# A conditional transformer chain on one core: tables with neutral rows, and a new order for late weights and masks

## The chip, the cores and the metric

The kernel runs on one core of a Trainium2 chip. A core has five engines with an instruction queue each: PE (matrix products), DVE (vector work), ACT (activations), POOL (GpSimd) and SP (here only for asking for transfers). Each engine takes its instructions in order. Sixteen DMA engines move data; transfers are asked for on the queues of SP, ACT and POOL. The metric is the time of one execution in device microseconds, the median of several runs.

## The reference

Four stages are applied one after the other to x, sixteen batch entries b of 256 tokens by 256 channels, in float32.

- Stage 0, an adapter with an expert for each b: `hidden = gelu(x @ down_W.T + down_b)`, then `hidden @ expert_W[id].T + expert_b[id]` where the id is valid (otherwise hidden is kept), plus an embedding, then `@ up_W.T + up_b`, plus x, and a layer norm with gain and offset.
- Stage 1, a transformer block with 16 heads of 16 channels: layer norm with a scale and a shift that come from a timestep (sine, cosine, silu, a 256x512 product); q, k, v; scores plus a bias of its own for every head (`fside`, 16 heads x 256 x 256 for each b), masked, softmax; projection; then a feed-forward net of 1024 channels with `x * sigmoid(1.702 x)`.
- Stage 2, one of three small nets for each b (two with two products, one with three), chosen by a condition 0, 1 or 2; nothing is added where the condition is something else; then a layer norm with gain and offset.
- Stage 3, one step of a two-dimensional finite-difference scheme: the field is multiplied by grids, differentiated along both axes (with one-sided forms at the edges), scaled by a dt for each b, added and clipped at zero.

In the inputs that are used every expert id and condition is valid, and condition 2 does not occur.

## The kernel before

Everything is done for one b after the other, with 128 rows on the partitions. Eight generators describe the stages: `prepare` (stage 0), `project` (q, k, v), `weigh` (scores, bias, softmax), `attend` (transposed probabilities times values, then `divide` and the projection), `enter` and `feed` (the feed-forward net), `end` (stage 2) and `step` (stage 3). A planner, `Flow`, runs when the program is built: it keeps an estimated clock for each engine and goes on with the generator that is ready and has the lowest position; `flow.add(gen, at, per)` gives each its starting position and how fast it advances. The order in which generators are resumed is the order of the instructions on each engine. Several stages of different b therefore interleave on PE.

In `weigh` the heads are taken in quads, 64 quads in all, four for each b. For each quad `load_side` asks SP for the 1 MB of biases (`side`, three buffers), and `add_mask` asks POOL for a transfer that adds the spread mask `neg` (made by `spread_mask` from the loaded mask) to the biases in place (L632). The softmax (L675 on DVE, exp at L686 on ACT) waits for that transfer. Before, quads 1 and 2 get their masks when quad 0 has been weighed, and quad m + 2 at the third head of quad m. `prepare` for b = 0 calls `timestep` after the first statistics and `condition` after the second ones.

Weights that are used later (w1, rows_b, w2, w_sr, grids: L185 on SP) are asked for at the start, behind the biases of quads 0 to 2. Expert weights are loaded by the id of each b (L279), and made neutral for an invalid id on POOL: multiplied by a valid flag (L486), and a diagonal `e_k` (L281) is added (L487). Branch weights of stage 2 are loaded by condition (L909), their last bias is multiplied by a valid flag (L989), and the product is multiplied by it as it is added (L1041).

`take_stats` makes mean and variance on DVE (L387, L388), and on POOL the inverse root `rs` (L391, L392) and `nb`, minus mean times rs (L394, L395). `normalized` applies them either on DVE (L402, without nb) or on ACT (L407, with nb), whichever engine's estimated clock is behind.

Of the kernel before, what the change touches and what calls it, by code (L numbers as in the profile page):

```python
# [11 lines left out]
F32 = mybir.dt.float32  # L12
BF16 = mybir.dt.bfloat16
I32 = mybir.dt.int32
# [5 lines left out]
P = 128  # L20
# [150 lines left out]
def chain_kernel(ctx: ExitStack, tc: tile.TileContext, t: dict, out: bass.AP):  # L171
# [57 lines left out]
    e_rows = load("e_rows", t["expert_rows"], [E, 2 * A])  # L229
# [21 lines left out]

    def steer(name, tok, n):

        f = fixed(f"{name}_f", [P, B])
        nc.vector.tensor_copy(f, tok)
        clip = fixed(f"{name}_clip", [P, B])
        nc.vector.tensor_scalar(clip, f, 0.0, float(n - 1), ALU.max, ALU.min)
        clip_i = fixed(f"{name}_clip_i", [P, B], I32)
        nc.vector.tensor_copy(clip_i, clip)
        valid = fixed(f"{name}_valid", [P, B])  # L260
        nc.vector.tensor_tensor(valid, clip, f, ALU.is_equal)
        return clip, clip_i, valid

    e_clip, e_idx, e_valid = steer("e", tok[:, :B], E)
    e_hot = small()
    nc.vector.tensor_scalar(e_hot, e_clip, columns("number"), None, ALU.is_equal)
    e_hot_valid = small()
    nc.vector.tensor_tensor(e_hot_valid, e_hot, e_valid, ALU.mult)

    e_keep = fixed("e_keep", [A, B])  # L270
    nc.vector.tensor_scalar(e_keep, e_valid[:A], -1.0, 1.0, ALU.mult, ALU.add)
# [3 lines left out]
    def load_expert(b):  # L275

        e = nc.sync.value_load(e_idx[0:1, b : b + 1], min_val=0, max_val=E - 1)
        w = xp.tile([A, A], F32, name=f"e_w{b}", tag="e_w")
        nc.sync.dma_start(out=w, in_=t["expert_W"][bass.ds(e, 1)].rearrange("e a o -> a (e o)"))  # L279
        keep = xp.tile([A, A], F32, name=f"e_k{b}", tag="e_k")  # L280
        nc.gpsimd.tensor_scalar(keep, ident[:A, :A], e_keep[:, b : b + 1], None, ALU.mult)  # L281
        e_ws[b] = w, keep

    load_expert(0)
    HB = 4
    sides = {}

    def load_side(m):
# [45 lines left out]
    def timestep():  # L334
# [4 lines left out]
        flow.dve(1.8)  # L339
        flow.act(3.5)  # L340
# [19 lines left out]

    load_mask(0)
    load_side(0)
# [3 lines left out]
    def later(name, src, shape):  # L366
        return load(name, src, shape, engine=nc.sync)

    load_side(1)
    wo = later("wo", chunked(t["Wo"]), [P, NC, D])  # L370
    load_side(2)
    w1 = later("w1", chunked(t["W1"]), [P, NC, F])
    rows_b = later("rows_b", rows(t["rows_b"]), [P, 3 * D + B])
    b2, ln3_g, ln3_b = (rows_b[:, i * D : (i + 1) * D] for i in range(3))
    dt = rows_b[:, 3 * D :]
    w2 = later("w2", chunked(t["W2"]), [P, NF, D])
    w_sr = later("w_sr", chunked(t["w_sr"]), [P, 6, D])
    w1_sr, w2_sr = w_sr[:, :NC, :], w_sr[:, NC:, :]
    grids = later("grids", chunked(t["grids"]), [P, NC, 7 * S])
# [3 lines left out]
    def take_stats(name, src, after):  # L383
# [9 lines left out]
        nb = xp.tile([P, NC], F32, name=f"nb{name}", tag="nb", bufs=12)  # L393
        nc.gpsimd.tensor_tensor(nb, mv[:, :, 0], rs, ALU.mult)  # L394
        nc.gpsimd.tensor_scalar(nb, nb, -1.0, None, ALU.mult)  # L395
        return (mv, rs, nb), flow.pool(1.65, at)

    def normalized(dst, src, stat):
        mv, rs, nb = stat
        if flow.clock["DVE"] <= flow.clock["ACT"]:  # L400
# [4 lines left out]
            return flow.dve(0.65)  # L405
        for c in range(NC):
# [3 lines left out]
        return flow.act(0.97)  # L410
# [47 lines left out]
    def expert_bias():  # L458

        ps_b = misc("ps_b", [A, B])  # L460
        nc.tensor.matmul(ps_b, e_rows[:, :A], e_hot_valid[:E], start=True, stop=False)
        nc.tensor.matmul(ps_b, e_rows[:, A:], e_hot[:E], start=False, stop=True)
# [3 lines left out]
    def condition():  # L466

        nc.vector.tensor_scalar(emb, emb, 0.5, None, ALU.mult)
        nc.vector.scalar_tensor_tensor(silu, th, 1.0, emb, ALU.add, ALU.mult)
        flow.dve(0.4)  # L470
# [10 lines left out]


    def prepare():
        for b in range(B):
            w, keep = e_ws.pop(b)
            nc.gpsimd.tensor_scalar(w, w, e_valid[:A, b : b + 1], None, ALU.mult)  # L486
            nc.gpsimd.tensor_tensor(w, w, keep, ALU.add)  # L487
            flow.pool(0.85)
# [15 lines left out]
            yield at  # L504
            ps_e = misc(f"a_e{b}", [A, S])
# [3 lines left out]
            yield free(f"a_e{b}", flow.dve(0.4, flow.pe(0.45)))  # L509
            ps_u = misc(f"a_u{b}", [P, NC, D])  # L510
# [4 lines left out]
            stat, at = take_stats(f"0_{b}", x, at)  # L515
            yield at, 0
            if b == 0:
                timestep()
# [4 lines left out]
            if b == 0:  # L523
                condition()
                for va in vas:
                    nc.gpsimd.memset(va, 0.0)
# [7 lines left out]
    def project():  # L534
        for b in range(B):
# [56 lines left out]
            free(f"c_k{b}", flow.act(0.73, at))  # L592
            yield 0.0
# [13 lines left out]
            va = vas[b % 2]  # L607
# [7 lines left out]
            sums = wp.tile([P, NC, H], F32, name=f"c_sum{b}", tag="c_sum")  # L615
            ready[b] = x_t, qz, k_t, va, sums
            at = free(f"c_v{b}", flow.dve(0.67, at))
            done.add(("prepare", b))
# [9 lines left out]

    def add_mask(m):

        both = [P, HB, NC * S]
        nc.gpsimd.dma_start(  # L632
            out=sides[m].rearrange("p (h c) k -> p h (c k)", h=HB),
            in_=negs[m // 4].rearrange("p c k -> p (c k)").unsqueeze(1).to_broadcast(both),
            accum_op=ALU.add,
        )
        return flow.pool(1.0) + 9.0

    def weigh():

        masked = {}
        at = 0.0
        for m, (b, half, par) in enumerate(QUADS):
            if m % 4 == 0:
                yield lambda: ("prepare", b) in done
            if m == 0:
                spread_mask(0)
                masked[0] = add_mask(0)
# [566 lines left out]
```

## Time and profile before

| | before |
|---|---|
| runs, us | 941.1, 944.49, 946.65 (median 944.49) |
| profiled execution, us | 943.58 |
| its span, us | 941.8 |
| mean granted clock of PE | 0.973 |
| PE busy | 857.3 us, 91% |
| DVE busy | 643.7 us, 68% |
| ACT busy | 562.3 us, 60% |
| POOL busy | 541.4 us, 57% |
| mask transfers (POOL's queue) | 64, landing after 8.2 us |
| biases (SP's queue) | 256 of 256 KB, landing after 4.8 us |

The span runs from the first to the last recorded instruction; the execution's time lies a little above it. "Busy" adds up instructions[...]. A time given for a line in the profile is that of one execution. An engine's idle time is named after what ended it.

### The profile page before, as it was taken

The numbers are of one execution on the slowest core, as the hardware profiler recorded it, in microseconds if no ns is written. First come the engines' busy times: TensorE is split into PE (matmuls) and PEld (weight loads), VectorE is DVE, ScalarE is ACT, GpSimd is POOL, SyncE is SP. The second block draws the span as 40 slices with busy tenths as digits, with TensorE's granted clock in tenths as the row PEclk, the third lists the DMA queues.
The fourth block names the chain that finished last, engine by engine and source line by source line (L and its number), as shares of the span: only waits on it lengthen the run. The fifth ranks groups of instructions, "written<-read, shape, count | busy, mean of one in ns | idle before, by whom it ended". The sixth has DMA issues, their size and how long they took to land. (4 is left out here: it accounts for less than half of the span.)

```text
span 941.8 us, 17596 instructions
## 1 busy us (share of the span) xinstructions
PE 857.3 (91%) x5684; PEld 652.6 (69%) x5684; DVE 643.7 (68%) x2173; ACT 562.3 (60%) x1538; POOL 541.4 (57%) x717
## 2 busy tenths in 40 slices
PE   3778996798999999999999999999999999899894
PEld 2446674576776877777777778777776777677773
DVE  4367774867868595867677685858766676868435
ACT  2357564567757575776757576767665464657340
POOL 2245423448747566665748566666754665464481
PEclk9879998899999999999999999999999999999997
DMA  9888776485777758685877768675866676783000
GB/s 300 268 216 212 193 185 171 118 201 150 204 188 186 194 162 216 162 229 152 208 187 189 192 176 219 185 198 150 200 179 181 167 191 177 209 229 93 12 29 23
DMA packets 128654, 167.20 MB, mean 178 GB/s; under 512 B 12509, under 2 KB 86318, under 8 KB 128558
## 3 DMA queue, kind: packets, MB, share of 16 engines
q0 software_dynamic: 33792, 67.11, 33.6%
q1 hardware_dynamic: 93552, 96.92, 32.7%
q10 hardware_dynamic: 1214, 1.99, 0.6%
q8 instruction: 48, 0.79, 0.3%
q14 instruction: 48, 0.39, 0.1%
HBM read 94.69 MB, written 4.19 MB: 105 GB/s over the span
## 5 line engine op out<-in xcount | busy, mean ns | idle before, releaser
L686 ACT ACTIVATE c_pr<-c_sc,c_mx 128x256 f32<-128x256 f32 x512 | 255.9, 501 | 184.0 <-DVE c_mx L675 182.6
L675 DVE CUSTOM_DVE_ANT_0 c_sc<-c_s,side 128x256 f32<-128x256 f32 x512 | 194.7, 419 | 36.0 <-PE c_s L657 11.7
L433 PE MATMUL c_pt<-ident,c_pr 128*128 128x128 f32 x1024 | 158.3, 284 | 16.3 <-ACT c_pr L686 13.4
L433 PEld LDWEIGHTS c_pt<-ident,c_pr 128*128 128x128 f32 x1024 | 116.6, 143 | 67.2 <-ACT c_pr L686 32.7
L632 POOL DMA_DIRECT2D side<-neg x64 | 85.8, 1349 | 126.2 <-DMA side<-in_side 63.6
L441 DVE COPY c_pts<-c_pt 128x512 f32<-128x512 f32 x208 | 139.8, 683 | 17.8 <-PE c_pt L433 17.4
L833 PE MATMUL d_f<-d_ht,w 128*128 128x256 f32 x512 | 124.2, 387 | 1.4 <-ACT c_pts L443 0.9
L863 PE MATMUL d_o<-w,d_z 128*128 128x256 f32 x512 | 117.4, 383 | 0.0
L391 POOL TENSOR_SCALAR rs<-mv 128x2 f32<-128x2 f32 x64 | 14.5, 226 | 165.9 <-DVE mv L388 155.6
L833 PEld LDWEIGHTS d_f<-d_ht,w 128*128 128x128 f32 x512 | 92.6, 192 | 18.0 <-issue 2.7
L863 PEld LDWEIGHTS d_o<-w,d_z 128*128 128x128 f32 x512 | 96.1, 192 | 12.6 <-issue 0.4
L686 ACT ACTIVATION_READ_ACCUMULATOR c_pr<-c_sc,c_mx 128x1 f32 x512 | 96.8, 189 | 0.0
L657 PE MATMUL c_s<-c_kt,c_qz 32*128 32x256 f32 x1024 | 87.7, 408 | 3.3 <-DVE e_o L1122 2.1
L732 PE MATMUL c_c<-c_pts,c_va 128*32 128x256 f32 x1024 | 76.8, 388 | 10.6 <-DVE c_pts L441 9.2
L657 PEld LDWEIGHTS c_s<-c_kt,c_qz 32*128 32x128 f32 x1024 | 54.0, 186 | 27.9 <-issue 15.5
L852 ACT ACTIVATE d_f<-d_z 128x512 f32<-128x512 f32 x64 | 38.6, 603 | 38.7 <-DVE d_z L849 38.1
L732 PEld LDWEIGHTS c_c<-c_pts,c_va 128*32 128x32 f32 x1024 | 30.6, 109 | 44.2 <-issue 19.0
L871 DVE SCALAR_TENSOR_TENSOR y<-d_o,y 128x256 f32<-128x256 f32 x32 | 13.6, 424 | 55.7 <-PE d_o L863 55.7
L1120 DVE TENSOR_TENSOR e_d<-e_d,e_y 128x256 f32<-128x256 f32 x32 | 13.8, 431 | 54.7 <-POOL e_y L1108 48.7
L392 POOL TENSOR_TENSOR rs<-rs,inv_sqrt 128x2 f32<-128x2 f32 x64 | 46.2, 722 | 5.3
L1116 PE MATMUL e_d<-e_b,grids 128*128 128x256 f32 x128 | 34.9, 396 | 12.8 <-DVE e_b L1094 9.1
L856 DVE SCALAR_TENSOR_TENSOR d_z<-d_f,d_z 128x512 f32<-128x512 f32 x64 | 43.6, 681 | 3.0 <-ACT d_f L852 3.0
(168 smaller groups left out, 1649.8 us busy)
## 6 DMA issues: line engine op xcount, KB each, us to landing
side<-in_side SPq DMA_DIRECT2D x256, 256.0 KB, 4.8
side<-neg POOLq DMA_DIRECT2D x64, 1024.0 KB, 8.2
x<-in_x SPq DMA_DIRECT2D x16, 512.0 KB, 6.5
d_w<-in_W_branch SPq DMA_DIRECT2D x16, 512.0 KB, 3.3
out<-e_o SPq DMA_DIRECT2D x16, 256.0 KB, 4.7
w<-in_W SPq DMA_DIRECT2D x2, 1024.0 KB, 7.8
d_bout<-in_bl_branch SPq DMA_DIRECT2D x16, 128.0 KB, 3.4
grids<-in_grids SPq DMA_DIRECT2D x1, 1792.0 KB, 15.2
```

The source lines that it names most:

```text
L392: nc.gpsimd.tensor_tensor(rs, rs, inv_sqrt, ALU.pow)
L433: nc.tensor.transpose(ps[:, k, c * P : (c + 1) * P], src[:, c, k * P : (k + 1) * P], ident)
L441: nc.vector.tensor_copy(dst, ps)
L632: nc.gpsimd.dma_start(out=sides[m].rearrange("p (h c) k -> p h (c k)", h=HB), in_=negs[m // 4].rearrange("p c k -> p (c k)").unsqueeze(1). ...
L657: nc.tensor.matmul(ps[i][:, c, :], qz[rows32, par, half, c * P : (c + 1) * P], k_t[rows32, half, :], start=True, stop=True,)
L675: nc.vector.tensor_tensor_reduce(out=sc[:, c, :], in0=ps[i][:, c, :], in1=sb[:, i * NC + c, :], scale=-1.0, scalar=3.0e38, op0=ALU.add, op ...
L686: nc.scalar.activation(pr[:, c, :], sc[:, c, :], AF.Exp, bias=mx[:, c : c + 1], scale=-1.0, accum_out=sums[:, c, h : h + 1],)
L732: nc.tensor.matmul(ps_c[32 * i : 32 * i + 32, :], va[:, k, 4 * half + i, 2 * par : 2 * par + 2, :].rearrange("p e d -> p (e d)"), turned[i ...
L833: nc.tensor.matmul(ps_f[:, i, :], w1[:, k, f * P : (f + 1) * P], h_t[:, k, :], start=k == 0, stop=k == NC - 1,)
L852: nc.scalar.activation(ps_f, z, AF.Tanh, scale=0.851)
L856: nc.vector.scalar_tensor_tensor(z, ps_f, 1.0, z, ALU.add, ALU.mult)
L863: nc.tensor.matmul(ps_o, us[f // 2][:, f % 2, c * P : (c + 1) * P], w2[:, f, :], start=f == 0, stop=f == NF - 1,)
```

## The change

- Expert and branch tables get a neutral row at both ends (an identity, zeros), and `steer` gives a row number from 0 to n + 1. POOL's multiplications by valid flags go away.
- `take_stats` no longer makes nb; `normalized` makes it on POOL if it picks ACT, and it picks DVE a little more readily.
- w1, rows_b and w2 are asked for behind the biases of quad 3, w_sr and grids behind those of quad 4.
- The masks of quads 0 to 2 are asked for together, after the second statistics of b = 0; that of a later quad `to` is asked for from the third head of quad to - 2 on, once POOL's estimated clock is past the expected arrival of its biases (`side_at`), and at the latest at the second head of quad to - 1.
- `timestep`, `condition` and the silu move forward in `prepare`, which starts earlier (its position goes from -2.69 to -3.29). `project` reports its q and k before v is made, and only `attend` waits for v.
- The product of the last b but one in `step` waits for the last `branch`; the last output is clipped and stored in two halves; the positions of the generators change.

```diff
-    e_rows = load("e_rows", t["expert_rows"], [E, 2 * A])
+    e_rows = load("e_rows", t["expert_rows"], [E + 2, 2 * A])
...
-        clip = fixed(f"{name}_clip", [P, B])
-        nc.vector.tensor_scalar(clip, f, 0.0, float(n - 1), ALU.max, ALU.min)
...
-        nc.vector.tensor_tensor(valid, clip, f, ALU.is_equal)
-        return clip, clip_i, valid
+        nc.vector.tensor_scalar(f, f, 1.0, 0.0, ALU.add, ALU.max)
+        row = fixed(f"{name}_row", [P, B])
+        nc.vector.tensor_scalar(row, f, float(n + 1), None, ALU.min)
+        row_i = fixed(f"{name}_row_i", [P, B], I32)
+        nc.vector.tensor_copy(row_i, row)
+        return row, row_i
...
-        keep = xp.tile([A, A], F32, name=f"e_k{b}", tag="e_k")
-        nc.gpsimd.tensor_scalar(keep, ident[:A, :A], e_keep[:, b : b + 1], None, ALU.mult)
-        e_ws[b] = w, keep
-
-    load_expert(0)
+        e_ws[b] = w
...
-    def load_side(m):
+    def load_side(m, after=0.0):
+        side_at[m] = after + 6.5
...
         nc.scalar.activation(th, emb, AF.Tanh, scale=0.5)
-        flow.dve(1.8)
-        flow.act(3.5)
+        at = flow.act(3.4, flow.dve(1.6))
+        nc.vector.tensor_scalar(emb, emb, 0.5, None, ALU.mult)
+        nc.vector.scalar_tensor_tensor(silu, th, 1.0, emb, ALU.add, ALU.mult)
...
     load_mask(0)
+    load_expert(0)
     load_side(0)
...
     def later(name, src, shape):
-        return load(name, src, shape, engine=nc.sync)
+        return fixed(name, shape), src
...
-    w1 = later("w1", chunked(t["W1"]), [P, NC, F])
-    rows_b = later("rows_b", rows(t["rows_b"]), [P, 3 * D + B])
+    LATER = {
+        0: [
+            later("w1", chunked(t["W1"]), [P, NC, F]),
+            later("rows_b", rows(t["rows_b"]), [P, 3 * D + B]),
+            later("w2", chunked(t["W2"]), [P, NF, D]),
+        ],
+        1: [
+            later("w_sr", chunked(t["w_sr"]), [P, 6, D]),
+            later("grids", chunked(t["grids"]), [P, NC, 7 * S]),
+        ],
+    }
...
-        nb = xp.tile([P, NC], F32, name=f"nb{name}", tag="nb", bufs=12)
-        nc.gpsimd.tensor_tensor(nb, mv[:, :, 0], rs, ALU.mult)
-        nc.gpsimd.tensor_scalar(nb, nb, -1.0, None, ALU.mult)
-        return (mv, rs, nb), flow.pool(1.65, at)
+        return (mv, rs, name), flow.pool(1.1, at)
...
-        if flow.clock["DVE"] <= flow.clock["ACT"]:
+        if flow.clock["DVE"] <= flow.clock["ACT"] + 0.3:
...
+        nb = xp.tile([P, NC], F32, name=f"nb{name}", tag="nb", bufs=4)
+        nc.gpsimd.tensor_tensor(nb, mv[:, :, 0], rs, ALU.mult)
+        nc.gpsimd.tensor_scalar(nb, nb, -1.0, None, ALU.mult)
+        at = flow.pool(0.56)
...
-            nc.gpsimd.tensor_scalar(w, w, e_valid[:A, b : b + 1], None, ALU.mult)
-            nc.gpsimd.tensor_tensor(w, w, keep, ALU.add)
...
             yield at
+            if b == 0:
+                spread_mask(0)
+                for va in vas:
+                    nc.gpsimd.memset(va, 0.0)
...
             yield free(f"a_e{b}", flow.dve(0.4, flow.pe(0.45)))
+            if b == 0:
+                timestep()
...
             stat, at = take_stats(f"0_{b}", x, at)
+            if b == 0:
+                condition()
             yield at, 0
-            if b == 0:
-                timestep()
...
             stat, at = take_stats(f"1_{b}", x, at)
             if b == 0:
-                condition()
-                for va in vas:
-                    nc.gpsimd.memset(va, 0.0)
+                masked.update((m, add_mask(m)) for m in range(SIDES))
...
             free(f"c_k{b}", flow.act(0.73, at))
...
+            done.add(("prepare", b))
...
-            done.add(("prepare", b))
+            done.add(("values", b))
...
-                for to in range(1, 3) if m == 0 else [m + 2] if m + 2 < len(QUADS) else []:
-                    if i == 2:
-                        if to % 4 == 0:
-                            spread_mask(to // 4)
+                to = m + 2 if i >= MASK_FROM else m + 1
+                if SIDES <= to < len(QUADS) and to not in masked:
+                    if to % 4 == 0 and to // 4 not in negs:
+                        spread_mask(to // 4)
+                    if to == m + 1 and i == MASK_BY or flow.clock["POOL"] > side_at[to]:
                         masked[to] = add_mask(to)
...
                 if i == 3 and m + SIDES < len(QUADS):
-                    load_side(m + SIDES)
+                    load_side(m + SIDES, at)
+                    for got, src in LATER.pop(m, []):
+                        nc.sync.dma_start(out=got, in_=src)
...
         for m, (b, half, par) in enumerate(QUADS):
+            if m % 4 == 0:
+                yield lambda: ("values", b) in done
...
-            nc.gpsimd.tensor_scalar(b_out, b_out, c_valid[:, b : b + 1], None, ALU.mult)
...
-            nc.vector.scalar_tensor_tensor(y, ps_o, c_valid[:, b : b + 1], y, ALU.mult, ALU.add)
-            at = free(f"d_y{b}", flow.dve(0.78, at))
+            nc.vector.tensor_tensor(y, ps_o, y, ALU.add)
+            at = free(f"d_y{b}", flow.dve(0.66, at))
...
             yield at_b
+            if b == B - 2:
+                yield lambda: ("branch", B - 1) in done
...
-                    nc.scalar.activation(o, o, AF.Relu)
+                if c or b == B - 1:
+                    nc.scalar.activation(o[:, part, :], o[:, part, :], AF.Relu)
...
-    flow.add(prepare(), -2.69, 2.25)
-    flow.add(project(), -2.29, 5.7)
+    flow.add(prepare(), -3.29, 2.25)
+    flow.add(project(), -2.21, 5.7)
     flow.add(weigh(), 0, 21.2)
-    flow.add(attend(), 1.04, 11.3)
-    flow.add(enter(), 1.41, 0.44)
-    flow.add(feed(), 3.57, 13.9)
-    flow.add(end(), 4.07, 3.95)
-    flow.add(step(), 3.96, 3.5)
+    flow.add(attend(), 1.8, 11.3)
+    flow.add(enter(), 0.5, 0.44)
+    flow.add(feed(), 3.86, 13.9)
+    flow.add(end(), 3.9, 3.95)
+    flow.add(step(), 5.33, 3.5)
...
-        "expert_W": l0["expert_W"].transpose(0, 2, 1),
+        "expert_W": np.concatenate([eye, l0["expert_W"].transpose(0, 2, 1), eye]),
```

## The prediction

> **What bounds the kernel.** I read the windows by stage first, then by 10 us, then what PE waited for, then the timeline of the first 70 us and of the end. The columns of a window row are its length, busy us of PE, PE's weight loads, DVE, ACT and POOL (instruction counts in brackets), granted PE clock, DMA share, GB/s.
>
> ```profile
> 0.00:100.00 100.00, 68.82 (x386) 46.58 (x387) 55.50 (x210) 47.11 (x122) 36.05 (x65) 0.90 0.87 250
> 100.00:200.00 100.00, 84.80 (x533) 61.18 (x532) 72.98 (x238) 58.44 (x155) 41.06 (x64) 0.93 0.63 160
> 200.00:800.00 600.00, 584.43 (x4016) 451.80 (x4015) 428.86 (x1460) 391.31 (x1082) 390.12 (x496) 1.00 0.72 187
> 800.00:942.00 142.00, 119.22 (x754) 93.08 (x752) 86.37 (x267) 65.45 (x181) 74.17 (x93) 0.95 0.36 98
> ```
>
> From 200 to 800 us PE is 97% busy, so 15.6 us is all that a better order can win there. PE's idle time lies outside: 31.2 us in the first 100, 15.2 in the second, 22.8 at the end. The work on PE is the same before and after, so the change must win there.
>
> ```profile
> 20.00:30.00 10.00, 8.81 (x29) 6.36 (x30) 4.93 (x24) 3.87 (x6) 7.36 (x11) 1.00 1.07 370
> 30.00:40.00 10.00, 8.78 (x42) 6.55 (x41) 1.75 (x4) 3.15 (x5) 0.00 (x0) 1.00 1.08 352
> 40.00:50.00 10.00, 4.95 (x20) 2.92 (x24) 6.62 (x24) 3.29 (x12) 3.94 (x7) 0.53 0.23 53
> 50.00:60.00 10.00, 6.09 (x40) 3.09 (x32) 4.85 (x20) 3.29 (x12) 4.03 (x7) 0.67 1.12 250
> 150.00:160.00 10.00, 3.71 (x31) 2.31 (x29) 6.03 (x23) 6.28 (x14) 1.38 (x4) 0.83 0.86 239
> 160.00:170.00 10.00, 8.43 (x43) 6.21 (x44) 2.53 (x7) 4.13 (x9) 3.70 (x5) 0.65 0.02 9
> ```
>
> The DMA engines are full to 40 us, and PE is then idle and at a low clock. The timeline (start, length, engine, instruction) says why:
>
> ```profile
> 23.70 2.39 SPq L185 DMA_DIRECT2D grids<-in_grids  x1
> 27.50 1.50 POOL L632 DMA_DIRECT2D side<-neg  x1 [0.32 <-POOL neg L358]
> 36.58 1.15 PE L657 MATMUL c_s<-c_kt,c_qz 32*128 32x256 f32 x16
> 42.78 0.42 DVE L675 CUSTOM_DVE_ANT_0 c_sc<-c_s,side 128x256 f32<-128x256 f32 x1 [5.27 <-issue]
> 47.43 2.67 POOL L632 DMA_DIRECT2D side<-neg  x2 [0.33 <-issue]
> 54.82 0.42 DVE L675 CUSTOM_DVE_ANT_0 c_sc<-c_s,side 128x256 f32<-128x256 f32 x1 [3.82 <-DMA side<-neg]
> ```
>
> The first mask is asked for at 27.5, behind 5 MB of late weights, and DVE can start the first softmax at 42.78, though its scores were ready at 37.7. The second mask is asked for at 47.4 and holds DVE again until 54.82.
>
> What PE waited for (total us, times, longest) gives the other two places:
>
> ```profile
> PE e_d L1116 <- DVE e_b L1094: 9.1, 1, 9.1
> PE d_g L1001 <- DMA d_w<-in_W_branch: 7.5, 1, 7.5
> PE a_e L506 <- POOL e_w L487: 3.4, 3, 1.5
> ```
>
> [...] masks land in 8.2 us in the middle, 15.2 at worst, and the first (issued to 29.0, used at 42.78) is near the worst. [...] 0.53 and 0.67 after the idle 5.1 us from 38.8 to 43.9; 0.65 after 7.5 idle us at 153.8.
>
> **Part 1, tables.** POOL loses L486 (0.44 to 0.97), L487 (0.31), L281 (0.44) and L989 (0.93) for each b, about 2.4 us x 16 = 38, and 50 of 64 nb pairs (0.20 + 0.23 each) = 21: 60 of its 541 us. POOL isn't the bound, so this is worth only what PE waited for it: a_e behind e_w, 3.4 us. L1041 becomes a plain addition (the nearest, L513, takes 0.69 against 0.74). Loads have the same bytes. Bounds 0 to -4; I take **-3**.
>
> **Part 2, the first 65 us.** I walk the new order with the old durations.
> - a_e needs only the load: 9.9 to 11.0 (was 10.62).
> - On DVE hid ends at 11.6, then the cosine's 1.6 us to 13.2, ACT's Sin, table load 1.28 and Tanh to 15.0, the two silu operations to 15.5. They stand ahead of the addition to x, which a_u could feed at about 14. With the stats: 17.4 (was 16.3).
> - PE's ps_a, 3.6 us, runs 15.5 to 19.1, and its four DVE copies stand ahead of the first layer norm, which starts at 19.35 (was 17.75). Norm 2.0, stats 1.15, rs 0.95: 23.5.
> - POOL issues three masks here, 1.35 to 1.5 each, 4.1 together, ahead of the nb that c_ln waits for. nb 0.5, c_ln 1.1: 29.4 (was 23.65). The masks' biases don't hold POOL: up to the third, 6.3 MB are asked for, at 354 GB/s some 21 us by my estimate from the windows.
> - ACT then has a table load 1.28, gelu 0.47 and c_xt 1.02: 32.2 (was 28.8). a_e and a_u of b=1 now stand ahead of c_q on a cold PE, 1.1 + 0.5 + 2.1, so c_q starts at 34.9 (was 28.7). The 7.9 us from c_q to c_s stay: c_s at 43, c_sc at 43.7, and behind b_tmp (1.1) and the table the first exp at 44.3. Before: 43.25. **So far the change loses 1 us.**
> - But now all three masks have landed: issued at 23.5 to 27.6, about 5 us of full engines each (33.6% of the span over 64), so by 29 to 41. Exps of quad 0 go 44.3 to 49.4; c_ln, table, gelu, table (4.1) follow; those of quad 1 go 53.5 to 58.5. Before they ran from 55.29 to 65.5. The last c_pt of quad 1 ends at about 63.4 (was 67.9), and c_q, c_k and c_v of b=1 (3 x 1.73) are done by then too, which they weren't before. Lead: 67.9 + 5.2 - 63.4 = 9.7.
>
> Bounds: -4, if a cold PE or one more late mask costs 5 us; -13, if the clock stays up. I take **-9.5**.
>
> **Part 3, late weights.** w1, rows_b and w2 (2.4 MB, about 7 us at 350 GB/s) follow side 3, w_sr and grids (2.6 MB) side 4. Behind them on SP stand x3, e_w3 and side 5. First uses: w1 at about 125 us, grids later; side 3's mask has 9.2 us of PE work from issue to use, side 4's 11.9. I cost it at nothing: the softmax of quads 1 to 3 hides it. Without that cover side 3's mask, sharing with w1 and w2, would land as late as the worst 15 us and hold DVE for 4. Bounds 0 to +4.
>
> **Part 4, masks in the middle.** The issue moves from two quads ahead to later ones. In PE work standing between issue and first use (0.216 us per 128x256 pass, 0.11 per transposition, 0.0625 per pass of c_s and c_c) the repeating leads are 12.8, 20.8, 19.0, 18.7, against 14.9, 20.9, 31.3, 25.7. Issue and landing need 1.35 + 8.2. So **0**; what stood behind POOL's 63.6 us of waiting for biases gets freer, bounds -4 to +15 (rival C).
>
> **Part 5, first branch weights.** d_w(0) is still asked for just before use, and now x and e_w stand between side 11 and it on SP: 0.4 + 1.3 + about 0.4 of transfer. The 7.5 us wait becomes 9.5: **+2**, bounds 0 to +4.
>
> **Part 6, the end.** Let C be the end of the last c_o. Before: C = 892.96, next d_t, d_g (2.2 us) covered the stats of b=15, and relu ended at C + 45.6. Now only d_y (1.73) stands there; d_ln goes to ACT and waits for nb, which stands on POOL behind e_p of b=13 (1.27) and rs of b=14 (1.0): stats C + 2.05, rs + 1.1, e_p + 1.3, rs + 1.1, nb + 0.5, d_ln + 1.1, so d_t at C + 7.1 instead of C + 3.6; d_ht then is uncovered, 1.1, and e_d of b=13 (3.46) stands between d_f. d_o ends at C + 25.8 instead of + 20.0. Then the new order wins: d_y, and y on DVE, no longer stand behind e_d of b=14, which held DVE until 922.95: 2 us back; the halved last output 0.5. Relu ends at about C + 48.5. C itself comes 0.6 earlier (1.3 us of PE work moved behind it, 0.7 new idle). Net **+2**, bounds -3 to +5.
>
> **Sum.** -3 - 9.5 + 0 + 0 + 2 + 2 = -8.5 on the profiled execution, 943.6 (span 941.8 and 1.8 around it): 935.1. The median 944.5 stands 0.9 above that execution: 936. I predict 935.
>
> **Rivals.**
> - A, more is won: PE stays warm from 30 us on, POOL's freed time shortens the middle. For it: 11 us of PE work at clocks of 0.53 and 0.67. Head -13, middle -6: 925. Against it: PE is idle from 21 to 29 in my own chain.
> - B, the lead is spent: c_ln behind three mask issues and the tail's nb are worth 4.1 + 5. If side 2 lands after 30, POOL's third issue and everything behind moves 4 us more. -4.5 + 2 + 2 = 943.
> - C, slower: masks come late in the middle. The shortest lead, 12.8, leaves 3.2 us after issue and landing. When POOL gets to its issue over 3.2 us late, behind two 1.3 us operations and a bias's landing, DVE stops in order, c_pt after it. 2 us in one of four quads and 1 in another is 45 us of DVE over 15 b, a third of it on PE: +15 - 8.5 = 950. Against it: in the profile DVE waited for a mask once in 64.
>
> **How the numbers follow.** Forecast 0.45 (929 to 940), A 0.19 (918 to 929), B 0.22 (940 to 948), C 0.14 (948 to 960). 0.5% is 4.7 us, about what a measurement of this kernel can tell from no change: faster is below 939.8, all of A and nearly all of the forecast, 0.63; same 0.22; slower 0.15. The range 921 to 951 leaves out the outer part of A and most of C above 951.
>
> **What would show it.** First c_sc near 43.7 and no DVE wait for a mask at quads 1 and 2; c_q of b=1 before 58; nb of b=0 after three mask issues; PE's wait for d_w near 9.5; PE idle some 6 us ahead of the last d_f. Wrong if DVE waits for masks recur from 200 us on, or PE's idle time in 60 to 200 grows.

## The result

The changed kernel takes 983.98 us (median of 982.92 to 986.06) against 944.75 (941.1 to 946.65): 1.0423 times as long, interval 1.0385 to 1.046. The forecast was 935, the range 921 to 951, and slower had a chance of 0.15, for another reason. The profiled execution has a span of 981.2 us against 941.8, 39.4 more. What follows is compared by spans where profiles are read and by medians where versions are. In the names of the tiles, a_ is the adapter, c_ attention, d_ the feed-forward net and the branch, e_ the finite differences; c_sc are the scores with their biases, c_pr their exps, c_ln and d_ln the layer norms ahead of attention and of the feed-forward net, and d_ht is the transposed input of the latter.

The windows by stage of the changed kernel (length, busy us of PE, its weight loads, DVE, ACT, POOL with counts, granted PE clock, DMA share, GB/s):

```profile
0.00:100.00 100.00, 72.58 (x408) 48.37 (x408) 58.88 (x220) 49.93 (x131) 32.77 (x50) 0.95 0.91 261
100.00:200.00 100.00, 82.89 (x519) 60.14 (x520) 69.12 (x231) 61.40 (x159) 33.94 (x43) 0.90 0.61 163
200.00:800.00 600.00, 563.89 (x3821) 431.27 (x3821) 446.34 (x1417) 357.59 (x1008) 326.11 (x364) 0.97 0.68 176
```

The first 100 us hold more PE work than before (408 instructions, not 386), so the head was won, by 4 us at its end. The middle holds 3821 instead of 4016, although POOL has 64 us less to do there. PE now idles 36 us where it had idled 15.6, and its clock is 0.97 instead of 1.00.

When DVE takes up the projection (y from c_o) of a b shows where it went. The second column is the start before, in us; the others are the difference to it, for the changed kernel and for some of the experiments below, and the last row compares the spans.

| b | before | changed | e1 | e6 | e12 | e11 | e13 | e18 |
|---|---|---|---|---|---|---|---|---|
| 0 | 101.2 | -4.0 | -2.7 | -3.2 | -2.5 | -3.5 | -7.9 | -8.5 |
| 3 | 274.9 | -3.9 | -3.2 | -4.3 | -3.7 | -4.5 | -9.8 | -18.9 |
| 9 | 590.2 | +8.6 | -8.0 | -9.1 | -8.6 | -5.0 | -11.5 | -21.2 |
| 10 | 642.1 | +16.9 | -0.5 | -3.5 | -6.8 | -5.0 | -11.1 | -20.5 |
| 11 | 693.3 | +28.2 | +11.0 | +4.0 | -4.0 | -5.1 | -11.1 | -20.6 |
| 15 | 893.2 | +31.8 | +1.2 | -6.0 | -12.4 | -5.5 | -11.3 | -22.0 |
| span | 941.8 | +39.4 | +9.1 | +1.9 | -8.4 | -5.8 | -11.5 | -22.7 |

The changed kernel is 4 us ahead at b = 0, loses 12.5 from b = 3 to 9 (some 2.1 per b), 19.6 in two steps at b = 10 and 11, 3.6 more by b = 15, and 7.6 after the last projection.

**Once per b.** What PE and DVE waited for (total us, times, longest); the waits of c_s for d_z and c_pts belong to the two steps further below:

```profile
PE a_h L503 <- DVE c_mx L677: 9.0, 5, 1.8
PE c_s L659 <- DVE c_mx L677: 7.8, 4, 2.4
PE c_s L659 <- DVE d_z L864: 6.4, 1, 6.4
PE c_s L659 <- DVE c_pts L447: 5.1, 1, 5.1
DVE c_sc L677 <- ACT c_pr L688: 35.0, 22, 3.6
```

No wait of DVE for a mask is left. Instead DVE stands for the exps (c_pr), 35.0 us where it was 6.8 in the kernel before:

```profile
DVE c_sc L675 <- ACT c_pr L686: 6.8, 6, 2.5
```

The timeline of ACT, DVE and PE at one such place (start, length, engine, line, instruction, in brackets the idle time before it and what ended it):

```profile
335.36 1.00 ACT L818 ACTIVATE d_ht<-d_t,cols 128x256 f32<-128x256 f32 x2
336.37 1.28 ACT L1017 ACT_TABLE_LOAD   x1
337.67 0.84 ACT L1017 ACTIVATE d_hid<-d_g,b_sel 128x256 f32<-128x256 f32 x2
338.61 1.28 ACT L688 ACT_TABLE_LOAD   x1
339.90 0.51 ACT L688 ACTIVATE c_pr<-c_sc,c_mx 128x256 f32<-128x256 f32 x1
341.03 0.42 DVE L677 CUSTOM_DVE_ANT_0 c_sc<-c_s,side 128x256 f32<-128x256 f32 x1 [3.56 <-ACT c_pr L688]
344.39 1.59 PE L503 MATMUL a_h<-x,w_down 128*64 128x256 f32 x4 [1.80 <-DVE c_mx L677]
```

From 335.36 to 339.90 ACT does d_ht, the branch's gelu and two table loads. The tile c_sc, which goes from DVE to the exp, has two buffers. Both are full, so DVE stands 3.56 us at the next c_sc, and with it all that follows in its queue. PE then waits 1.80 us at a_h, until DVE's c_mx has read scores: in the program both take their PSUM tiles from the same seven. In the kernel before, d_ht stands 5 us behind the gelu, and from 488 to 500 us DVE stops for 0.68 us at most:

```profile
490.89 0.84 ACT L1010 ACTIVATE d_hid<-d_g,b_sel 128x256 f32<-128x256 f32 x2
496.15 1.00 ACT L810 ACTIVATE d_ht<-d_t,cols 128x256 f32<-128x256 f32 x2
```

That d_ht directly ahead of the gelu is what fills the buffers is read from these timelines; it was not tried by itself. The planner books engines, PSUM banks and the six c_pr tiles, but not the two buffers of c_sc: the DVE of its plan runs on.

**The two steps.** DVE, POOL and PE at 622 us:

```profile
622.12 1.36 POOL L488 DMA_DIRECT2D side<-neg  x1 [0.30 <-POOL neg L352]
622.30 7.15 DVE L404 TENSOR_SCALAR c_ln<-x,mv,rs 128x256 f32<-128x256 f32 x2
...
623.01 1.77 POOL L1105 TENSOR_TENSOR e_p<-y,grids 128x512 f32<-128x512 f32 x1
...
624.24 1.76 POOL L1108 TENSOR_TENSOR e_m<-y,grids 128x512 f32<-128x512 f32 x1
...
628.04 1.26 POOL L1115 TENSOR_TENSOR e_y<-e_y,e_v 128x508 f32<-128x508 f32 x1
630.10 2.08 PE L659 MATMUL c_s<-c_kt,c_qz 32*128 32x256 f32 x12 [5.12 <-DVE c_pts L447]
```

A pair of c_ln takes 0.73 us for b = 2 to 6 and 1.07 for b = 9 to 13; here it takes 7.15, until POOL's row of five grid operations of `step` is through (the last starts at 628.04 and takes 1.26). It happens again:

```profile
682.58 7.19 DVE L404 TENSOR_SCALAR c_ln<-x,mv,rs 128x256 f32<-128x256 f32 x2
```

The first operation of the pair takes 5.83 of the 7.15 us (5.87 of the 7.19). It starts while POOL asks for a mask, 0.7 us ahead of the row, and ends at 628.13, behind the first gap in the row: of the first four grid operations each starts before the one ahead of it has ended (623.01 for 1.77 us, then 624.24), and only the fifth, which reads what the fourth wrote, starts after it. POOL's recorded times are rough, but the other pair goes the same way: the mask is asked for at 682.43 (1.37 us), the first normalization runs from 682.58 to 688.45, and the fifth grid operation starts at 688.37, 0.08 us after the fourth has ended. So the mask's issue may be part of what holds DVE; no run parts it from the row.

All 96 normalizations on DVE (L404) take 64.8 us, where the kernel before had 94 in 39.0.

### The profile page after: what moved, and what is told of

Read it like the earlier page. It is cut to its first block, busy times and chain, and to the rows that moved or that the text cites. A ratio compares the mean times of both kernels' runs of the same rounds, so it can differ in the third digit from the quotient of the medians.

```text
span 981.2 us, 17414 instructions
## 1 busy us (share of the span) xinstructions
PE 874.8 (89%) x5684; PEld 661.6 (67%) x5684; DVE 680.7 (69%) x2196; ACT 547.1 (56%) x1514; POOL 483.5 (49%) x553
## 5 line engine op out<-in xcount | busy, mean ns | idle before, releaser
L677 DVE CUSTOM_DVE_ANT_0 c_sc<-c_s,side 128x256 f32<-128x256 f32 x512 | 193.7, 417 | 43.7 <-ACT c_pr L688 35.0
L439 PE MATMUL c_pt<-ident,c_pr 128*128 128x128 f32 x1024 | 147.7, 279 | 13.2 <-ACT c_pr L688 10.0
L439 PEld LDWEIGHTS c_pt<-ident,c_pr 128*128 128x128 f32 x1024 | 114.1, 141 | 53.5 <-ACT c_pr L688 29.6
L841 PE MATMUL d_f<-d_ht,w 128*128 128x256 f32 x512 | 131.4, 403 | 1.5 <-ACT d_ht L818 0.7
L841 PEld LDWEIGHTS d_f<-d_ht,w 128*128 128x128 f32 x512 | 99.1, 202 | 25.3 <-DVE c_pts L447 2.6
L431 POOL TENSOR_TENSOR e_tmp<-e_tmp,rows_b 128x512 f32<-128x512 f32 x15 | 19.1, 1271 | 196.1 <-DVE e_tmp L404 196.1
L659 PE MATMUL c_s<-c_kt,c_qz 32*128 32x256 f32 x1024 | 85.3, 413 | 19.7 <-DVE c_mx L677 7.8
L857 DVE TENSOR_SCALAR d_z<-d_f,cols 128x256 f32<-128x256 f32 x100 | 43.5, 477 | 12.2 <-PE d_f L841 11.4
L593 ACT ACTIVATE c_qz<-c_q,bqz,cols 128x256 f32<-128x256 f32 x32 | 16.3, 560 | 62.3 <-DVE c_qz L589 62.3
```

The source lines that it names most:

```text
L439: nc.tensor.transpose(ps[:, k, c * P : (c + 1) * P], src[:, c, k * P : (k + 1) * P], ident)
L659: nc.tensor.matmul(ps[i][:, c, :], qz[rows32, par, half, c * P : (c + 1) * P], k_t[rows32, half, :], start=True, stop=True,)
L677: nc.vector.tensor_tensor_reduce(out=sc[:, c, :], in0=ps[i][:, c, :], in1=sb[:, i * NC + c, :], scale=-1.0, scalar=3.0e38, op0=ALU.add, op ...
L841: nc.tensor.matmul(ps_f[:, i, :], w1[:, k, f * P : (f + 1) * P], h_t[:, k, :], start=k == 0, stop=k == NC - 1,)
L857: nc.vector.tensor_scalar(z[:, i, :], ps_f[:, i, :], b1[:, f : f + 1], None, ALU.add)
```

## Experiments

### The first mechanism: two buffers of c_sc (e1)

```diff
-                sc = hp.tile([P, NC, S], F32, name=f"c_sc{m}_{i}", tag="c_sc", bufs=2)
+                sc = hp.tile([P, NC, S], F32, name=f"c_sc{m}_{i}", tag="c_sc", bufs=4)
```

> The changed kernel with four c_sc buffers in place of two, order unchanged. Theory 1 (once per b DVE stops in order, with two c_sc full, until ACT has got through d_ht, a table load, the branch's gelu and the table load back, 3.6 us; PE then stands 1.8 us ahead of a_h): DVE's wait for c_pr falls from 35 us to under 8, PE's a_h wait from 9.0 to under 2, and 2 us in each of 8 to 10 repeats come back with what the lower clock cost: 964 to 970. Rival (ACT is late in any case, the wait only moves to the next buffer or to PE's c_pt): within 4 us of 984.

952.63 us, 31 less than the changed kernel, and 1.0089 (1.0059 to 1.0118) of the kernel before. The gain is larger than expected: the waits of DVE for c_pr and of PE's a_h for c_mx are gone from the list of waits, and from b = 3 to 9 the kernel now wins 4.8 where it lost 12.5. PE's two waits for c_mx had added up to 16.8 us; how much of the rest is the lower clock behind them (0.97 in the middle, now 0.99) was not parted. The gelu and the two table loads are still there; only DVE's freedom to run ahead of them is new. The window of the middle holds 3983 of PE's instructions where the changed kernel had 3821 and the kernel before 4016:

```profile
200.00:800.00 600.00, 580.17 (x3983) 447.40 (x3982) 460.96 (x1472) 369.60 (x1048) 337.21 (x374) 0.99 0.70 183
```

The order on every engine is that of the changed kernel, so theory 1 is shown as far as the two buffers go. The two steps remain (+7.5 and +11.5).

### What held c_ln (e2, e5, e6, e7)

e2 and e5 move c_ln of two b from DVE to ACT (the lines left out are ACT's two activations), with the bookings left as they were. This is e5; e2 names 1_11 and 1_12:

```diff
         if flow.clock["DVE"] <= flow.clock["ACT"] + 0.3:
+            if name in ("1_14", "1_15"):
+                nb = xp.tile([P, NC], F32, name=f"nb{name}", tag="nb", bufs=4)
+                nc.gpsimd.tensor_tensor(nb, mv[:, :, 0], rs, ALU.mult)
+                nc.gpsimd.tensor_scalar(nb, nb, -1.0, None, ALU.mult)
...
+                return flow.dve(0.65)
```

> The changed kernel with the second layer norm's c_ln of b = 11 and 12 on ACT (with its nb on POOL) instead of on DVE; the planner books the same costs, so all else keeps its place. Theory 2 (these two DVE operations, 7.15 and 7.19 us for a pair that takes 0.73 elsewhere, are held by POOL's five grid operations in a row, and PE stands behind them for 5.1 and 6.4 us and then runs at a lower clock): the two stalls at 620 and 680 vanish, and 14 to 20 us come back: 964 to 970. Rival (DVE is late there for another reason, or ACT, with 1.1 us and a wait for nb more, holds PE as long): 978 to 985.

992.11 us (1.046 to 1.0595): 8 slower, with two runs near 987 and two near 997. I had taken the wrong two. `prepare` runs some four b ahead, and the held pairs are those of b = 14 and 15; those that e2 moved had taken 1.07 us. So it tells something else, what a c_ln costs on ACT when nb is made only then:

```profile
PE a_e L529 <- ACT a_h L514: 11.3, 5, 4.7
```

> The changed kernel with c_ln of b = 14 and 15 on ACT (nb on POOL), the planner booking the same costs. These are the two that took 7.15 and 7.19 us on DVE (e2_cln_act moved two others, which had taken 1.07, and lost 8 us). Theory 2 (POOL's grid operations hold them, PE stands behind them): the stalls at 620 and 680 go, 14 to 20 us come back less some 4 each for an a_h that now waits for ACT, as in e2: 968 to 976. Rival (the time is lost there anyway): 981 or more.

977.13 us, 7 less than the changed kernel, not 14 to 20. The held pairs are gone, but now nb waits on POOL behind the same grid operations, and ACT waits for it 2.1 us, twice. Theory 2 holds in part: the stall goes with the held pairs, but moving them makes ACT late.

> Four c_sc buffers and c_ln of b = 14 and 15 on ACT, both in the changed kernel. If the two mechanisms are separate, their gains add: 952.6 less what e5 shows against 984, by the theory 934 to 945, so level with the kernel before or ahead. If e1 had already taken up what the held operations cost: 950 to 955.

946.6 us, 1.0036 (1.0024 to 1.0048): the gains of e1 (31) and e5 (7) add up to within a microsecond. Two separate mechanisms.

e7 measures the disputed cost by itself:

```python
for _ in range(6):
    nc.gpsimd.tensor_tensor(w, x, u, ALU.mult)
for _ in range(8):
    nc.vector.tensor_scalar(z[:, :256], x[:, :256], col[:, 0:1], col[:, 1:2], ALU.subtract, ALU.mult)
```

> A kernel of its own that computes nothing of the reference (it writes zeros): eight equal DVE operations of 128x256 each, alone or beside six POOL tensor_tensor of 128x512 in a row, all in SBUF. Theory 2 (a DVE operation with one SBUF source and two pointer scalars waits until POOL's row of operations is through): tensor_scalar alone 0.41 us each, beside POOL the eight take as long as POOL's six, 7 to 8 us. bn_stats, and the same tensor_scalar with its source in PSUM, keep 0.41 to 0.48 us. tensor_tensor and scalar_tensor_tensor with two SBUF sources are held too. Rival (POOL doesn't hold DVE; it was a semaphore that the trace doesn't show): all stay at 0.41 to 0.5.

Its timeline, eight DVE operations to a line, alone and beside POOL's six:

```profile
7.69 3.55 DVE L45 TENSOR_SCALAR z<-x,col 128x256 f32<-128x256 f32 x8 [3.06 <-issue]
12.91 8.83 DVE L45 TENSOR_SCALAR z<-x,col 128x256 f32<-128x256 f32 x8 [1.66 <-ACT x L75]
13.01 8.13 POOL L69 TENSOR_TENSOR w<-x,u 128x512 f32<-128x512 f32 x6 [11.26 <-ACT x L75]
23.41 3.66 DVE L49 BATCH_NORM_STATS2 st<-x 128x6 f32<-128x256 f32 x8 [1.68 <-ACT x L75]
33.09 9.29 DVE L53 TENSOR_TENSOR z<-x,u 128x256 f32<-128x256 f32 x8 [6.02 <-ACT x L75]
43.17 4.61 DVE L57 TENSOR_SCALAR z<-ps,col 128x256 f32<-128x256 f32 x8 [0.78 <-ACT x L73]
44.18 7.96 POOL L69 TENSOR_TENSOR w<-x,u 128x512 f32<-128x512 f32 x6 [2.53 <-ACT x L75]
53.73 9.41 DVE L61 SCALAR_TENSOR_TENSOR z<-x,col,u 128x256 f32<-128x256 f32 x8 [5.96 <-ACT x L75]
53.84 8.50 POOL L69 TENSOR_TENSOR w<-x,u 128x512 f32<-128x512 f32 x6 [1.70 <-ACT x L75]
74.50 3.64 DVE L53 TENSOR_TENSOR z<-x,u 128x256 f32<-128x256 f32 x8 [11.35 <-ACT x L75]
```

As expected: eight operations of the normalization's form take 3.55 us alone and 8.83 beside POOL, a tensor_tensor with two SBUF sources 3.64 and 9.29, and a scalar_tensor_tensor with two took 9.41 beside POOL, while eight bn_stats take 3.66 beside POOL, 0.46 each. The same tensor_scalar with its source in PSUM took 4.61, 0.58 each, all but the first 1.0 us of it beside POOL. POOL loses less: its six take 8.13 us beside the normalization, 8.44 beside the tensor_tensor and 8.50 beside the scalar_tensor_tensor, against 7.98 beside bn_stats and 7.96 beside the operations on PSUM. What in an operation decides whether it is held was not shown: bn_stats, too, has a single source and its result in SBUF, and was not held. One thing differs from the kernel: if the 5.28 us of delay here fall on six of the eight normalizations, one for each of POOL's operations, each of those takes some 1.3 us (an estimate from 8.83 and 3.55), while in the kernel one c_ln took 5.87 us, through four grid operations. POOL's six all write w, while of the four in the kernel each starts before the one ahead of it has ended. Whether that makes the difference was not tried.

### Is d_ln on ACT the trigger? (e9, e12)

```diff
+        if name.startswith("2_"):
...
+            return flow.act(0.97, flow.pool(0.56))
         nb = xp.tile([P, NC], F32, name=f"nb{name}", tag="nb", bufs=4)
```

> The changed kernel with every d_ln on DVE, as in the kernel before, the planner booking the same costs, so all else keeps its place (two c_sc buffers). Theory 3: what sets off the stall that four c_sc buffers take away is d_ln on ACT for b = 3 to 10 and 15 (the new rule for the engine picks ACT there, and nb, made only then, holds ACT 1.4 us more): ACT gets to the exps behind it 2.4 us late in the repeats that lose 2 us, and not in those of b = 11 to 14, where d_ln is on DVE. Then DVE's wait for c_pr falls from 35 to under 12 us and PE's a_h wait of 1.8 us goes; with the 4.6 us of the last d_ln at the end: 956 to 966. Rival (d_ht, gelu and the two table loads, 4.4 us in a row on ACT, are enough for the stall by themselves): 974 to 982, the end alone.

977.4 us: theory 3 falls. DVE's wait for c_pr is as in the changed kernel:

```profile
DVE c_sc L683 <- ACT c_pr L694: 34.4, 22, 3.6
```

The starts of the projections, too, agree with those of the changed kernel to 1.2 us at every b. The left-out lines of the diff do the normalization on DVE. Only the end gains (6 us of the span), where d_ln of b = 15 waited for nb.

e12 adds three things up: four c_sc buffers, d_ln on DVE, and c_ln of b = 14 and 15 on ACT with nb made right behind rs, in `take_stats`:

```diff
+    EARLY, early = ("1_14", "1_15"), {}
...
+        if name in EARLY:
+            early[name] = nb = xp.tile([P, NC], F32, name=f"nb{name}", tag="nb", bufs=4)
+            nc.gpsimd.tensor_tensor(nb, mv[:, :, 0], rs, ALU.mult)
+            nc.gpsimd.tensor_scalar(nb, nb, -1.0, None, ALU.mult)
         return (mv, rs, name), flow.pool(1.1, at)
```

> The changed kernel with four c_sc buffers, every d_ln on DVE, and c_ln of b = 14 and 15 on ACT with their nb made right behind rs. Against e6 (946.6) the nb no longer stands behind a grid operation, 2 us twice, and the end's 4.6 us with its low clock goes: 934 to 941, ahead of the kernel before. If d_ln on DVE is held by POOL there: 945 or more.

935.55 us, 0.9911 (0.9881 to 0.9942): ahead of the kernel before, and 48 below the changed one, with its order on PE, its masks and its tables. So most of the loss comes back without another order. The steps at b = 10 and 11 shrink to +1.8 and +2.8.

### Which edit makes the order? (e3, e4, e10, e14, e15, e16)

e3 gives the changed kernel the old starting points, e4 the kernel before the new ones:

```diff
-    flow.add(prepare(), -3.29, 2.25)
-    flow.add(project(), -2.21, 5.7)
+    flow.add(prepare(), -2.69, 2.25)
+    flow.add(project(), -2.29, 5.7)
...
-    flow.add(step(), 5.33, 3.5)
+    flow.add(step(), 3.96, 3.5)
```

> The changed kernel with the seven starting points of the planner's chains (prepare to step) as in the kernel before. If the new starting points make the order that stalls: per-b time in the middle back to 52 or 53 us from 54.7, no DVE normalization over 3 us, 940 to 950. If the operations themselves (tables, nb, masks) or other placing rules do it: 970 or more.

993.02 us (1.049 to 1.057), worse: PE waits 19.3 us for c_pts, and a c_ln pair is held for 8.51 us.

> The kernel before with the new starting points alone. If these make the order that stalls: 960 to 990, with the same once-per-b stall. If they need the other edits for it: 940 to 950.

959.14 us (1.0136 to 1.0233): the new starting points cost the kernel before 15 us, by other waits (DVE 18.5 for two masks, 11.2 for c_pr). e3 falls under the second reading of its expectation (970 or more: not the starting points alone). e4 lies a little below the range of its first, and its stalls are other ones.

```diff
-        return (mv, rs, name), flow.pool(1.1, at)
+        nb = xp.tile([P, NC], F32, name=f"nb{name}", tag="nb", bufs=12)
...
+        return (mv, rs, nb), flow.pool(1.65, at)
...
-        if flow.clock["DVE"] <= flow.clock["ACT"] + 0.3:
+        if flow.clock["DVE"] <= flow.clock["ACT"]:
```

> The changed kernel with the kernel before's rule for the engine of a layer norm, its nb made at once for each, and the costs booked for them; the planner then orders everything anew. By theory 3 d_ln goes back to DVE, and the stall with it: 945 to 962. If another edit makes the order that stalls (masks' placing, starting points): 970 or more.

971.38 us (1.0265 to 1.0343): d_ln does not go back to DVE, as was expected (ACT does it for 8 of the 16 b, for 9 in the changed kernel, for none in the kernel before). DVE's wait for c_pr is 9.1 all the same, but three pairs of c_ln are held for 6.3 us each. Another order, other places.

```diff
-                to = m + 2 if i >= MASK_FROM else m + 1
-                if SIDES <= to < len(QUADS) and to not in masked:
...
+                for to in [m + 2] if 1 <= m and m + 2 < len(QUADS) else []:
+                    if i == 2:
...
-        return flow.pool(1.0, side_at[m]) + 9.0
+        return flow.pool(1.0) + 9.0
```

> The changed kernel with the masks from quad 3 on placed by the old rule (two quads ahead, behind the third pair), the rest as changed; the planner orders anew. If the bookings by the biases' arrival make the order that stalls: 940 to 955, DVE's wait for c_pr under 12. If the order comes from many small bookings: 960 to 1000, with stalls at other places.

976.24 us. The middle is the same as in the changed kernel (waits of 33.3 for c_pr, c_ln pairs of 7.14 and 7.18), and at b = 15 it is 31.1 behind the kernel before, not 31.8. Nearly all of the 8 us come back after the last projection, where DVE, and not ACT, now does d_ln of b = 15.

```diff
-            done.add(("prepare", b))
             yield 0.0
...
-            done.add(("values", b))
+            done.add(("prepare", b))
...
-            if m % 4 == 0:
-                yield lambda: ("values", b) in done
```

> The changed kernel with the scores of a b waiting for its values too, as in the kernel before (one flag, set behind c_v); the planner orders anew. If the earlier start of the scores is what piles four c_sc behind ACT: 940 to 955. Otherwise 960 to 1000.

984.2 us. The order on PE, DVE and ACT is that of the changed kernel, instruction for instruction, so this edit moves nothing here.

e16 is e3 with `bufs=4` for c_sc.

> The kernel of e3_old_starts (993.0) with four c_sc buffers. There DVE waits 29.4 us for c_pr, PE 19.3 for c_pts and 17.1 for c_pr. If two c_sc buffers are what makes any order of the planner's slow: 955 to 970. If that order is slow for other reasons: over 980.

982.84 us against 993.0 in e3: DVE's wait for c_pr falls from 29.4 to 1.1, and only 10 us come back. So two c_sc buffers are not what makes every order slow; there the waits for c_pts (16.9) and the held pair (8.80) remain.

e14 and e15 rule two edits out. The starting points and the layer norms' rule each change the order; neither taken back restores the old one. What the planner's bookings of the tables and of the head do to it was not tried apart.

### What the operations are worth in the old order (e8, e11, e13, e17, e18)

In these five, the costs are booked as in the kernel before, so that PE, DVE and ACT run in its order.

e8 is the kernel before with `bufs=3` for c_sc.

> The kernel before with three c_sc buffers [...]. There DVE waits only 6.8 us for c_pr, so by theory 1 little is to be had: 940 to 945. If more c_sc buffers help whatever the order is, since they let DVE run ahead of the exps: 915 to 932.

940.57 us, 0.9964 (0.9941 to 0.9987). c_sc's depth is worth 31 us in the new order and 3.6 in the old.

e11 takes the hunks of the change that belong to the tables, without their bookings, such as

```diff
-            w, keep = e_ws.pop(b)
-            nc.gpsimd.tensor_scalar(w, w, e_valid[:A, b : b + 1], None, ALU.mult)
-            nc.gpsimd.tensor_tensor(w, w, keep, ALU.add)
+            w = e_ws.pop(b)
             flow.pool(0.85)
```

> The kernel before with the tables alone (the neutral rows, and the operations that they save on POOL and DVE), the costs booked as before, so its order is kept. By the prediction's part 1: -3 us, 940 to 943; POOL's busy time falls by 38 us. If a POOL that is less busy runs its grid operations closer together and holds DVE's layer norms with them: 945 to 955.

935.86 us, 0.9916 (0.9889 to 0.9942): 8 us, more than I had expected. POOL's busy time falls from 541.4 to 505.9. Of the 5.8 us of the span 3.5 are there at b = 0.

e13 adds, to the tables, the early masks (the spread mask behind a_h of b = 0, the three transfers behind its second statistics) and the late weights:

```diff
             if b == 0:
+                spread_mask(0)
...
+                for m in range(SIDES):
+                    add_mask(m)
...
                     load_side(m + SIDES)
+                    for got, src in LATER.pop(m, []):
+                        nc.sync.dma_start(out=got, in_=src)
```

> The kernel before with the tables, the first three masks asked for in the prologue and the late weights behind sides 3 and 4; every cost is booked where and as it was, so PE, DVE and ACT run in the order of the kernel before (to be read against e11_tables, 935.9). By the prediction's part 2 the wait at 54.82 goes and the first exps start some us sooner: 4 to 9 us below e11, 927 to 932. If the head's lead is spent before the middle (in the changed kernel 15 us at 60 us were 4 at 97): 933 to 937.

931.25 us, 0.9855 (0.9816 to 0.9893): 4.6 below e11. Its timeline has the first softmax at 36.84 instead of 42.78, and the lead of 7.9 at b = 0 is kept to the end:

```profile
36.84 0.42 DVE L679 CUSTOM_DVE_ANT_0 c_sc<-c_s,side 128x256 f32<-128x256 f32 x1 [0.23 <-PE c_s L661]
```

e17 is e13 with `bufs=3` for c_sc.

> e13 (931.3) with a third c_sc buffer. e8 gave 0.4% in the kernel before, where DVE waits 6.8 us for c_pr; here it waits 8.2: 926 to 930 if a third buffer takes up that wait, 930 to 932 if it is hidden.

928.29 us, 0.9849 (0.9821 to 0.9877): not to be told from e13, whose ratio is 0.9855 with much the same interval. e18 is e17 with the first branch weights asked for earlier:

```diff
                         nc.sync.dma_start(out=got, in_=src)
+                    if m == 1:
+                        load_branch(0)
...
             if b == 0:
-                load_branch(0)
                 b1_sel = chosen["b1"]
```

> e17 with the first branch weights asked for behind side 4 and the grids instead of just before their use (the order on PE, DVE and ACT is the same). By the prediction's part 5 the wait of PE for them (6.8 us in e13) goes, and with it the low clock behind it: 7 to 10 us below e17, 917 to 923. If another transfer, or what comes behind it in the order (the values' biases, side 5), holds PE at that place: 925 or more.

921.14 us, 0.977 (0.9738 to 0.9801), 63 below the changed kernel. The wait for d_w, in e17 still

```profile
PE d_g L1006 <- DMA d_w<-in_W_branch: 6.7, 1, 6.7
```

is gone in e18, and 7.1 of the expected 7 to 10 us come back.

## Why the prediction was wrong

**The step that failed is part 4, and the sentence that it rests on: "From 200 to 800 us PE is 97% busy, so 15.6 us is all that a better order can win there".** That bounds a gain, and I used it as if it bounded the change: of the new order I priced the masks' leads alone, at 0 (-4 to +15), and the rest of the order at nothing. The changed kernel is at 984; the tables, masks and late weights in the old order are at 931 (e13). So the rest of the change, the new order with the late nb and the moved timestep in it, costs about 50 us. Of these the runs show 31 as DVE's wait for two c_sc buffers (e1), 7 as the two held pairs of c_ln, net of what ACT then loses (e5, e6), and, with the last d_ln and an earlier nb, 48 in all (e12). I had seen the new order on each engine, but asked of it only when masks are issued, not what each in-order engine does while the next stands.

- **Part 1, tables, -3 (0 to -4).** Measured -8.0 in the median, -5.8 in the span (e11). Right in sign, too small; the wait of a_e for e_w (3.4) was the whole of my estimate, and the rest is not explained.
- **Part 2, the head, -9.5.** The chain held to within about 1.3 us: c_q at 35.33 (predicted 34.9), the first c_sc at 42.90 (43.7), c_q of b = 1 at 54.28 (before 58). These are the lines, with the three masks asked for together:

```profile
24.07 4.12 POOL L488 DMA_DIRECT2D side<-neg  x3
35.33 3.03 PE L574 MATMUL c_q<-c_xt,w_qkv 128*128 128x256 f32 x8
42.90 0.42 DVE L677 CUSTOM_DVE_ANT_0 c_sc<-c_s,side 128x256 f32<-128x256 f32 x1 [0.30 <-PE c_s L659]
54.28 1.89 PE L574 MATMUL c_q<-c_xt,w_qkv 128*128 128x256 f32 x8
```

  c_v of b = 1 starts at 57.74 where it had started at 72.91. But the lead was assumed to last. From 70 to 90 us PE does 82 instructions at clocks of 0.76 and 0.73, where it did 143 at 0.93 and 1.00, and by the first projection 4 us are left. The two slices of the changed kernel, then those of the kernel before:

```profile
70.00:80.00 10.00, 6.29 (x35) 3.46 (x36) 5.64 (x22) 8.09 (x21) 2.31 (x3) 0.76 1.08 354
80.00:90.00 10.00, 9.36 (x47) 6.58 (x42) 5.97 (x20) 3.75 (x12) 4.73 (x5) 0.73 1.11 319
70.00:80.00 10.00, 9.14 (x69) 6.83 (x68) 6.05 (x21) 6.19 (x20) 6.38 (x7) 0.93 0.73 176
80.00:90.00 10.00, 7.35 (x74) 4.37 (x74) 8.44 (x34) 8.16 (x22) 4.01 (x8) 1.00 0.81 226
```

  In the old order, with the timestep's part left where it was, 4.6 were kept (e13 against e11).
- **Part 3, late weights, 0.** There is no wait of DVE for a mask or of PE for these weights, but 0 is not shown. From 60 to 90 us the DMA engines' share is 1.10 where it was 0.79. POOL stands at the mask of quad 4 until its biases have landed, rs of the next c_ln stands behind that mask, and DVE and PE wait in turn, just where the lead goes:

```profile
71.24 1.31 POOL L488 DMA_DIRECT2D side<-neg  x1 [4.68 <-DMA side<-in_side]
73.67 0.73 DVE L404 TENSOR_SCALAR c_ln<-x,mv,rs 128x256 f32<-128x256 f32 x2 [2.59 <-POOL rs L397]
74.22 0.78 PE L439 MATMUL c_t<-ident,c_ln 128*128 128x128 f32 x4 [2.04 <-DVE c_ln L404]
```

  That mask lands at 82.6 us, where it had landed at 82.5. How much of this is the late weights' was not tried apart.
- **Part 5, first branch weights, +2.** Right: 10.2 us instead of 7.5. e18 shows that this wait is on the path.
- **Part 6, the end, +2.** From the end of the last c_o to the end of the last relu it was 53.6 us where it had been 45.6, so +8. d_t came at C + 6.5 (predicted 7.1), behind d_ln, which waited for nb:

```profile
930.66 1.09 ACT L413 ACTIVATE d_ln<-y,nb,rs 128x256 f32<-128x256 f32 x2 [7.85 <-POOL nb L410]
```

  What I left out is that d_f and e_d of b = 13 then run at a lower clock, 0.66 from 930 to 940 us (d_o ends at C + 28.7, predicted 25.8). And e_d of b = 14 did not move out of the way of the last y: its four DVE operations now stand behind the statistics of y instead of ahead of y, so the 2 us did not come back. With d_ln on DVE (e9) 5.7 of the 8 are gone.
- **The rivals.** A and B did not happen. C had the right sign and place, DVE stopped in order in the middle, once per b, but the wrong mechanism: no mask was late. What stood ahead of DVE was its own output buffer. Of the signs of being wrong, the second came, if weakly: PE's idle time from 60 to 200 us grew from 20.7 to 22.0.

## What to carry to other kernels

A re-ordered in-order program has to be priced engine by engine where it was full before: a stage with 97% on one engine can lose far more than the 3% that it can win, and what a planner doesn't book (here the depth of one small tile, 31 us in e1, and what DVE's operations cost beside POOL's, 8.83 us for 3.55 in e7) is where this one lost. Change operations first in the old order, with the old bookings, to see what they are worth; then the order. If an order stalls at many places, look for the shallowest tile between two engines before looking for the edit.

## What I had not expected of the hardware

Eight DVE normalizations took 8.83 us beside POOL's elementwise row in e7, where alone they took 3.55, and a single one up to 5.87 in the kernel, where the median c_ln takes 0.41; eight bn_stats (3.66) and eight operations on PSUM (4.61) were not held, and POOL lost 2 to 7% (8.13 to 8.50, against 7.98 beside bn_stats). And c_sc's depth was worth what the order made of it: one buffer more (2 KB for each partition) 3.6 us in the old order (e8), two more 10 us in one new order (e16 against e3) and 31 in another (e1).
